# One decoder layer on one core: the shared expert's upper matrices as seven block products, and a rearranged end

## The chip, the cores and the metric

The kernel runs on one NeuronCore of one Trainium2 chip. The metric is the device time of one execution in microseconds (us), and the number that counts is the median over executions. All data are float32, but for the two operands of one small product that the reference itself rounds to eight bits; those are kept in bfloat16. Engines are named as in the profile: PE (TensorE, the matrix unit), PEld (its weight load), DVE (VectorE), ACT (ScalarE), POOL (GpSimd), SP (SyncE, which here only issues transfers).

## The reference

Inputs are `x` (4 x 512 tokens x 512 features), `ctx` (4 x 512 x 512) and weights. Three residual steps follow each other:

```python
x = x + attention(layernorm(x))     # 32 query heads, 8 key/value heads of 64, rotary, causal; wq, wk, wv, wo
x = x + xattn(layernorm(x), ctx)    # both rounded to fp8 in blocks of 128, then a 512 x 512 product per batch
x = x + ffn(layernorm(x))

def ffn(xt):                        # xt: 2048 tokens x 512;  H = 704, E = 8 experts
    probs = softmax(xt @ Wg); eidx = argmax(probs); gate = probs[eidx]
    pos = running count of earlier tokens with the same eidx; keep = pos < 256
    xd[eidx*256 + pos] = xt         # kept rows scattered into 8 x 256 slots
    oe = (silu(xd @ W1) * (xd @ W3)) @ W2           # each expert on its own 256 slots
    out = oe[eidx*256 + pos] * gate * keep          # gathered back, per token
    shared = (silu(xt @ sw1) * (xt @ sw3)) @ sw2    # every token, the "shared expert"
    return out + shared
```

The change is about the line `shared` and about the last lines of the program, in which `out` is gathered and added.

## The kernel before, in words

**Stages.** The four batches go through the attention one after another; the projections, the output product, the cross attention (jobs `c`, `s`, `t`) and the third norm with the routing (job `w`) are generators ("jobs") that a small planner, `Fill`, interleaves with the attention's own matmuls. Each job has a due step, a cost in ns of PE time, and jobs it must follow; a job yields after each piece of PE work, or with a wish to wait a while, or until DVE has room ("dve") and POOL is thought idle ("quiet"). The planner keeps a modelled time, `work.at`. All this only fixes the order in which instructions are written down; on the chip each engine runs its own list in that order, and waits for semaphores.

**Job `t`** (one tile of 128 tokens of the cross attention): DVE normalises the tile and takes block maxima (L251, L460), POOL scales it (L442), DVE rounds it in four passes (L449 to L456), PE transposes it (`ptr_h`), and four products `py` (L602) follow, each weighted by DVE (`y`, L604, in one of two buffers tagged `qm`) and added to `acc` by POOL (L597). **Job `w`**: statistics, norm, transposes (`ptr_h`, L641) with a copy to DRAM (`h3d`), the router's product `plg`, DVE's small routing arithmetic, the count product `pc`, and four indirect transfers on POOL that scatter the rows into `xd` (L719).

**Shared expert.** When the last batch's attention is done, units of the shared expert fill PE while that batch's jobs finish: `shared_up(b, c)` computes, for batch b and one block c of 128 hidden features, two products of 512 tokens over four blocks k of 128 features (8 matmuls of 128x512; block 5 holds the remaining 64 features of both matrices and has 4). ACT applies silu, DVE multiplies. `shared_down(b, j)` makes two tiles of 128 tokens of the lower product (12 matmuls of 128x512), and DVE adds them to rows `xt` that were loaded from `x2`. `between()` gives the planner a turn after every second matmul. A batch's transposed input `h3x` is loaded back from `h3d`, in two alternating buffers. The planner's loop ends when all jobs are done (L1271).

**Experts.** Expert e takes its 256 rows `xe` from `xd` (SP), transposes them, runs the same `up` on 256 columns and `down`, and stores `oe`. Weights alternate between two slots, loaded by SP behind the previous expert (the first by ACT, L1165).

**End.** In the kernel before, 27 of the shared expert's 32 units come ahead of the experts, the last of them just ahead of expert 0's first unit; the other five (three upper units, one of them the half one, and two lower ones) run behind expert 7. Sixteen gathers (L1350, POOL, one for each tile of 128 tokens) fetch the expert rows, four at a time, with a reload of `xt` from `x2` each, and DVE combines them (L1358); then SP stores the output (L1363, L1252).

PSUM has eight banks: four tagged `sp` (scores, `up`, `down` of the shared expert), one `av`, three `mm` (all jobs). A tag's banks are taken in turn, so a product waits until its predecessor in that bank has been read.

Of the kernel before, what the change touches and what calls it, by code (L numbers as in the profile page):

```python
# [14 lines left out]
P = 128  # L15
# [8 lines left out]
def decoder_layer(  # L24
# [453 lines left out]

    def pace(b):

        return 1 if b < B - 1 else 0.5

    cscales = {}

# [264 lines left out]
    for b in range(B):  # L749
        z = b * SPB  # L750
        before = [(("acc", b - 2), 0.7)] if b > 1 else []
        add(z + 5, 0, ("x", b), load(load_x, b), *before)
        if b:
            add(z - 18, 0, ("wv", b), load(load_v, b), (("q", b - 1, 11), 0.5))
            add(z - 24, 0, ("hx", b), load(load_h, b), *([(("zero",), 0.7)] if b == 1 else []))
            add(z - 22, 0, ("hs", b), job_hs(b), (("hx", b), 1))
            add(z - 16, 1760, ("h", b), job_h(b), (("hs", b), 1.5), (("q", b - 1, 4 * NG - 1), 0))
        for j in range(TB):
            if b or j:
                add(  # L760
                    z - 16, MM4, ("v", b, j), job_v(b, j), (("h", b), 0.2), (("wv", b), 1.5),
                    want=z - 4 + 0.8 * j,
                )
        for a in range(NG):
            za = z + 10 * a
            if za:
                if a == 0:
                    before = ("q", b - 1, 4 * NG - 1)
                else:
                    before = ("q", b, 4 * a - 5) if a > 1 else ("v", b, TB - 1)  # L770
                n = b * NG + a
                add(
                    za - 20, 0, ("wk", b, a), load(load_k, b, a),
                    *([(("k", *divmod(n - 2, NG)), 0.5)] if n > 2 else []),
                )
# [27 lines left out]
        before = [(("t", b - 1, j), 0) for j in range(TB)] if b else []  # L803
        add(z + 6, 220, ("cs", b), job_cs(b), *([(("w", b - 2), 0.7)] if b > 1 else []))
        add(z + (22 if b else 12), 4 * 220, ("c", b), job_c(b), (("cs", b), 0.2), *before)
        ze = z + SPB + 5
        add(ze, 0, ("s", b), job_s(b), (("o", b, NG - 1), 1))
        for j in range(TB):
            add(
                ze + 2 + (1, 3, 3, 2)[B - 1 - b] * j, 8 * 220, ("t", b, j), job_t(b, j),  # L810
                (("s", b), 0), (("c", b), 1), *([(("t", b, j - 2), 0)] if j > 1 else []),
            )
        add(ze + 9, 4 * 440 + 4000, ("w", b), job_w(b), *[(("t", b, j), 1) for j in range(TB)], *([(("cs", b + 1), 0)] if b < B - 1 else []))
    add(8, 0, ("zero",), job_zero())
    jobs.sort(key=lambda x: x.rank())
    for key in [("h", 0)]:
# [338 lines left out]
    ctx.enter_context(c_g)  # L1155
    se[1] = gp
    load_h3(1)
    slots = [gp.tile([P, WSLOT], F32, name="slot_e0")]
    evw = {}

    def job_e0():
        for evw[0] in load_ffn(slots[0], W1[0], W3[0], W2[0], bulk):
            yield -1

    add(n + 8, 0, ("e0",), job_e0())  # L1165
    jobs.sort(key=lambda x: x.rank())
    gTs, xts = {}, {}

# [33 lines left out]
    def down(gT, w2, t, name, tag, mid=None):  # L1202
# [22 lines left out]
            )  # L1225
        return pys

    def shared_up(b, c, mid=None):
        if c == 0:
            gTs[b] = gp.tile([P, NHC, T], F32, tag="gT", bufs=2, name=f"gT_{b}")  # L1230
        up(se["w"][0], h3x[b], gTs[b], c, T, f"s{b}_{c}", mid)
        if c == NHC - 1:
            se["next"] = b + 2
            load_h3(b + 2)

# [9 lines left out]
    def shared_down(b, j, mid=None):  # L1245
        for i in range(b * TB + j, b * TB + j + 2):
            xtile(i)
        for k, py in enumerate(down(gTs[b], se["w"][1], j, f"ys_{b}_{j}", "sp", mid)):
            i = b * TB + j + k
            nc.vector.tensor_tensor(xts[i], py, xts[i], ALU.add)  # L1250
            if i in routed:
                nc.sync.dma_start(out=outf[i * P : (i + 1) * P, :], in_=xts[i])  # L1252
            else:
                nc.sync.dma_start(out=x2[i * P : (i + 1) * P, :], in_=xts[i])
                routed_later.append(i)

    routed_later = []
    units = []
    for b in range(B):
        units += [(shared_up, b, c) for c in range(1 if b else 0, NHC)]  # L1260
        if b < B - 1:
            units.append((shared_up, b + 1, 0))
        units += [(shared_down, b, j) for j in range(0, TB, 2)]


    def between():
        work.at += 1720
        work.upto(n, 1e18, 2.8)

    between()  # L1270
    while jobs or work.now:  # L1271
# [3 lines left out]
        f(*args, between)  # L1275
        if se["next"] >= B - 1:
            load_h3(B - 1)
    c_am2.close()
    c_bp.close()
    c_acc.close()  # L1280

# [4 lines left out]
    def load_e(e):  # L1286
        if e < E:
            for evw[e] in load_ffn(slots[e % 2], W1[e], W3[e], W2[e], nc.sync.dma_start):
                pass

    xes, xTs, egTs = {}, {}, {}

    def load_rows(e):
        if e < E:
# [5 lines left out]

    def turn_rows(e):
        if e < E:
            xTs[e] = ep.tile([P, KC, CAP], F32, tag="xT", bufs=2, name=f"xT_{e}")
            for t in range(CT):
                nc.scalar.copy(
                    xTs[e][:, :, t * P : (t + 1) * P],
                    transpose4(xes[e, t], f"ptr_e_{e}_{t}"),
                )

    def expert_up(e, c):  # L1310
        if e < E:
            if c == 0:
                egTs[e] = ep.tile([P, NHC, CAP], F32, tag="egT", bufs=2, name=f"egT_{e}")
            up(evw[e][0], xTs[e], egTs[e], c, CAP, f"e{e}_{c}")

    load_rows(0)
    load_rows(1)
    for _ in range(3):
        f, *args = units.pop(0)
        rows_ahead(units)  # L1320
        f(*args)
    load_e(1)
    turn_rows(0)
    f, *args = units.pop(0)
    f(*args)
    expert_up(0, 0)
    for e in range(E):
        for c in range(1, NHC):
            expert_up(e, c)
            if c == 2:  # L1330
                turn_rows(e + 1)
                load_rows(e + 2)
        expert_up(e + 1, 0)
        for t, py in enumerate(down(egTs[e], evw[e][1], 0, f"epy_{e}", "mm")):
            yo = ep.tile([P, D], F32, tag="yo", bufs=2, name=f"yo_{e}_{t}")
            nc.vector.tensor_copy(yo, py)
            r0 = e * CAP + t * P
            nc.sync.dma_start(out=oe[r0 : r0 + P, :], in_=yo)
        load_e(e + 2)


    f, *args = units.pop(0)
    f(*args)

    ogs = {}

    def gather(i):
        xtile(i)
        ogs[i] = ep.tile([P, D], F32, tag="og", bufs=8, name=f"og_{i}")
        nc.gpsimd.indirect_dma_start(  # L1350
            out=ogs[i],
            out_offset=None,
# [9 lines left out]
        if last:  # L1362
            nc.sync.dma_start(out=outf[i * P : (i + 1) * P, :], in_=xts[i])  # L1363

    while units or routed_later:

        fresh = [
            (i, False)  # L1370
            for g, *a in units[1:2]
            if g is shared_down
            for i in range(a[0] * TB + a[1], a[0] * TB + a[1] + 2)
        ]
        while routed_later and len(fresh) < 4:
            i = routed_later.pop(0)
            xts.pop(i, None)
            fresh.append((i, True))
        for i, last in fresh:
            gather(i)  # L1380
        if units:
            f, *args = units.pop(0)
            f(*args)
        for i, last in fresh:
            combine(i, last)
    assert len(routed) == NT


# [58 lines left out]
```

## Time and profile before

| what | value |
|---|---|
| median of 3 runs | 1593.04 us (1593.01 to 1597.26) |
| the profiled execution's own time | 1592.05 us |
| its span in the trace | 1590.3 us (1.75 us lie around it) |
| PE busy | 1554.0 us of the span |
| DVE, ACT, POOL busy | 822.6, 515.0, 333.4 us |
| last attention product ends, first shared matmul begins | 1074.6 us |
| expert 0's first matmul | 1303.6 us |
| expert 7's last matmul ends | 1540.2 us |
| last matmul of all ends | 1577.0 us |

How to read it: a time in a row is counted from the span's start. A matmul of the program is two PE instructions (two passes over the float32 weights), so `x8` in a PE row is four matmuls. A row of the timeline gives start, duration, engine, line and operation, and in brackets how long the engine had been idle before and what ended that. In a table of windows, PEclk is the granted TensorE clock (1.00 is full).

### The profile page before, as it was taken

The page shows a single profiled execution, that of the slowest core. Times are in us where ns is not written, and L with a number is a line of the kernel's source. Part 1 is how long each engine was busy: PE and PEld are TensorE (multiplying, and loading weights), DVE is VectorE, ACT ScalarE, POOL GpSimd, SP SyncE. Part 2 cuts the span into 40 slices and gives each one's busy share as a digit, 9 for nine tenths or more (in the row PEclk, how much of TensorE's full clock was granted, in tenths as well). Part 3 has the DMA queues.
Part 4 walks back from the last instruction along what each step waited for, and adds up shares of the span by engine and source line. Part 5 has one row for each costly group of instructions (what it writes and reads, how often), then busy time and mean ns, then how long its engine had stood idle before and what let it go on. Part 6 is the DMA issues. An engine that isn't in the chain of part 4 may idle for free.

```text
span 1590.3 us, 19839 instructions
## 1 busy us (share of the span) xinstructions
PE 1554.0 (98%) x6664; PEld 853.4 (54%) x6664; DVE 822.6 (52%) x2399; ACT 515.0 (32%) x1541; POOL 333.4 (21%) x293
## 2 busy tenths in 40 slices
PE   8999999999999999999999999999999999999996
PEld 5455555545545555554555555554444557777752
DVE  4465843467776576887646686572454211111113
ACT  2354453434444444444444444441100201101100
POOL 2022301213343031333403034141132000000003
PEclk9999999999999999999999999999999999999998
DMA  4474431534325253443525423264241263556418
GB/s 140 125 225 143 100 100 30 149 100 100 99 63 153 78 140 114 100 110 93 130 61 153 131 69 83 72 204 127 77 141 66 66 205 121 157 170 232 140 61 283
DMA packets 118918, 195.32 MB, mean 123 GB/s; under 512 B 17184, under 2 KB 36640, under 8 KB 118304
## 3 DMA queue, kind: packets, MB, share of 16 engines
q10 hardware_dynamic: 65472, 100.94, 22.9%
q1 hardware_dynamic: 50784, 84.72, 17.4%
q0 software_dynamic: 2560, 8.39, 1.6%
q8 instruction: 53, 0.87, 0.2%
q14 instruction: 49, 0.40, 0.1%
HBM read 136.07 MB, written 28.57 MB: 104 GB/s over the span
## 4 chain that ended last, share of the span: by engine, by line
PE 87%; DMA 4%; DVE 3%; POOL 2%; ACT 1%; issue 1%; SPq 1%; ACTq 0%; DVEq 0%; POOLq 0%
PE py L408 14%; PE psq L308 13%; PE p_e L1181 10%; PE p_s L1181 9%; PE sc L939 8%; PE av L1020 8%; PE pt L989 7%; PE epy L1209 4%; PE psv L350 4%; PE ys L1209 3%; PE psk L308 3%; PE ptr_h L257 1%; DMA xt<-x 1%; DMA tsq<-t2q 1%; ACT pm L972 1%
## 5 line engine op out<-in xcount | busy, mean ns | idle before, releaser
L972 ACT ACTIVATE pm<-pm,mn 128x256 f32<-128x256 f32 (+3 forms) x512 | 280.9, 550 | 383.2 <-DVE mn L962 357.6
L962 DVE CUSTOM_DVE_ANT_0 pm<-sc,mask 128x256 f32<-128x256 f32 (+3 forms) x512 | 216.6, 486 | 91.0 <-PE sc L939 90.8
L408 PE MATMUL py<-wo,aT 128*128 128x512 f32 x512 | 240.3, 603 | 4.6 <-POOL aT L273 2.2
L308 PE MATMUL psq<-hT,wq 128*128 128x512 f32 x512 | 236.5, 599 | 2.3 <-DVE y L604 2.3
L1006 DVE COPY pT<-pt 128x128 f32<-128x128 f32 (+3 forms) x256 | 114.2, 485 | 114.2 <-PE pt L989 105.7
L939 PE MATMUL sc<-kT,t1q 64*128 64x384 f32 (+3 forms) x1024 | 165.8, 448 | 6.3 <-ACT pT L1000 2.5
L273 POOL TENSOR_TENSOR t1q<-t1q,tsq 128x512 f32<-128x512 f32 x64 | 83.1, 1298 | 391.8 <-DMA tsq<-t2q 214.2
L989 PEld LDWEIGHTS pt<-ident,pm 128*128 128x128 f32 x1280 | 143.7, 141 | 36.8 <-issue 27.8
L1181 PE MATMUL p_s<-h3x,slot_s 128*128 128x512 f32 x352 | 157.2, 596 | 0.0
L1181 PE MATMUL p_e<-xT,slot_e 128*128 128x256 f32 x704 | 155.1, 380 | 0.0
L989 PE MATMUL pt<-ident,pm 128*128 128x128 f32 x1280 | 154.5, 273 | 0.7 <-DVE mn L962 0.5
L1020 PE MATMUL av<-pT,v 128*64 128x512 f32 (+3 forms) x1024 | 152.4, 439 | 1.7 <-ACT pT L1000 1.7
L308 PEld LDWEIGHTS psq<-hT,wq 128*128 128x128 f32 x512 | 91.9, 190 | 102.1 <-issue 96.2
L408 PEld LDWEIGHTS py<-wo,aT 128*128 128x128 f32 x512 | 92.1, 191 | 99.7 <-issue 88.8
L1181 PEld LDWEIGHTS p_e<-xT,slot_e 128*128 128x128 f32 x704 | 132.6, 190 | 23.2 <-issue 5.8
L1000 ACT COPY pT<-pt 128x128 f32<-128x128 f32 (+3 forms) x256 | 97.1, 430 | 144.4 <-PE pt L989 114.7
L939 PEld LDWEIGHTS sc<-kT,t1q 64*128 64x128 f32 x1024 | 84.8, 186 | 87.1 <-issue 58.4
L1020 PEld LDWEIGHTS av<-pT,v 128*64 128x64 f32 x1024 | 68.3, 136 | 108.3 <-issue 96.2
L273 POOL TENSOR_TENSOR acc<-acc,y 128x512 f32<-128x512 f32 x64 | 80.9, 1269 | 180.6 <-DVE y L604 148.8
L1181 PEld LDWEIGHTS p_s<-h3x,slot_s 128*128 128x128 f32 x352 | 65.1, 190 | 74.8 <-issue 73.1
L972 ACT ACTIVATION_READ_ACCUMULATOR pm<-pm,mn 128x1 f32 x512 | 95.6, 187 | 0.0
L273 POOL TENSOR_TENSOR aT<-aT,rrb 128x512 f32<-128x512 f32 x64 | 81.0, 1296 | 30.5 <-DMA rrb<-rrd 30.5
(172 smaller groups left out, 1355.0 us busy)
## 6 DMA issues: line engine op xcount, KB each, us to landing
slot_e<-in_L_ffn_W_dram SPq DMA_DIRECT2D x14, 1280.0 KB
wq<-in_L_attn_wq_dram ACTq DMA_DIRECT2D x16, 1024.0 KB
tsq<-t2q SPq DMA_DIRECT2D x256, 64.0 KB
wo<-in_L_attn_wo_dram ACTq DMA_DIRECT2D x16, 1024.0 KB
rrb<-rrd ACTq DMA_DIRECT2D x32, 512.0 KB
slot_e<-in_L_ffn_W_dram SPq DMA_DIRECT2D x7, 1408.0 KB
kT<-t1k ACTq DMA_DIRECT2D x64, 128.0 KB
xt<-x SPq DMA_DIRECT2D x28, 256.0 KB
```

What stands on the lines that cost most here:

```text
L273: nc.gpsimd.tensor_tensor(*args)
L308: nc.tensor.matmul(ps, w[:, k, c0 : c0 + P], hTs[b][:, k, :], start=(k == 0), stop=(k == KC - 1),)
L408: nc.tensor.matmul(py, aT[:, r, j * P : (j + 1) * P], wts["o", a][:, r, :], start=(r == 0), stop=(r == 3),)
L939: nc.tensor.matmul(scs[g][:, o : o + nk], qTs[b, p][g * HD : (g + 1) * HD, it * P : nk], kTs[b, p // 2][g * HD : (g + 1) * HD, 0:nk], star ...
L962: nc.vector.tensor_tensor_reduce(out=pm[:, o : o + nk], in0=scs[g][:, o : o + nk], in1=mask[:, T - nk : T], scale=-(HD**-0.5), scalar=3.0e ...
L972: nc.scalar.activation(pm[:, o : o + nk], pm[:, o : o + nk], AF.Exp, bias=mn, scale=-1.0, accum_out=rss[b, a][:, col : col + 1],)
L989: nc.tensor.transpose(pt[:, j * P : (j + 1) * P], pms[g][:, j * P : (j + 1) * P], ident)
L1000: nc.scalar.copy(pT[:, 0 : it + 1, it * P : nk], pt[:, o : o + nk].rearrange("p (j t) -> p j t", t=P),)
L1006: nc.vector.tensor_copy(pT[:, it + 1, 0:nk], pt[:, o : o + nk])
L1020: nc.tensor.matmul(av[g * HD : (g + 1) * HD, j * P : T], vs[b][:, j, v0 : v0 + HD], rhs, start=(j == 0), stop=(j == TB - 1),)
L1181: nc.tensor.matmul(pp[:, 0:cols], w13[:, k, o : o + P], xT[:, k, 0:cols], start=(k == 0), stop=(k == KC - 1),)
L1209: nc.tensor.matmul(py, gT[:, c, (t + i) * P : (t + i + 1) * P], w2[:, c, :], start=(c == 0), stop=False,)
```

## The change

**1. Seven products instead of eight.** For batches 1 to 3 and hidden blocks 0 to 4 (15 chunks), `up7` replaces `up`. The two weight matrices' columns of the chunk (w1 on top, w3 below) and the two halves of the features make a 2 x 2 block matrix A; the features' halves and the tokens' halves make a 2 x 2 block matrix B. Strassen's scheme in Winograd's form gives the four blocks of A·B from seven products of blocks and sums of blocks. Each product is two matmuls of 128x256. The weight sums (s1 to s4, four POOL subtractions or additions of 2x128 columns per block) are made once, behind batch 0's use of the block; s1 overwrites a part of the weights. The token sums (t1 to t4, four POOL operations of 2x256) are made per batch, in `shared_down(b - 1, 0)`. Of the outputs, ACT copies two from PSUM, DVE makes five additions with a PSUM operand, POOL two additions of 256 columns and the final product of 512; silu is applied to the two halves.

**2. Order.** Block 5 of a batch now comes between its predecessor's two lower units. Of the lower units only the last three run behind expert 7; the upper ones are all ahead of the experts. The slot of expert 0's weights moves to where attention buffers were, and is loaded once the last output product is done. In the expert stage the transposed rows and the products live in parts of `h3x` and `wS`, which are free by then.

**3. End.** All `xt` rows are fetched ahead of expert 7's lower product, into buffers that are free; the 16 gathers go to POOL in a row behind the first lower unit's matmuls; the gathered rows go into the free weight slot.

**4. Planner.** In the last batch the jobs' wishes to wait are 0.3 of the others' instead of 0.5, the jobs `s` and `t` are due five steps earlier and the first two tiles at once; job `w` is due four steps earlier in all batches, which shifts a few matmuls in the attention's order too.

```diff
-        return 1 if b < B - 1 else 0.5
+        return 1 if b < B - 1 else 0.3
...
-        ze = z + SPB + 5
+        ze = z + SPB + (5 if b < B - 1 else 0)
...
-                ze + 2 + (1, 3, 3, 2)[B - 1 - b] * j, 8 * 220, ("t", b, j), job_t(b, j),
+                ze + 2 + (0, 3, 3, 2)[B - 1 - b] * j, 8 * 220, ("t", b, j), job_t(b, j),
...
-        add(ze + 9, 4 * 440 + 4000, ("w", b), job_w(b), *[(("t", b, j), 1) for j in range(TB)], *([(("cs", b + 1), 0)] if b < B - 1 else []))
+        add(ze + 5, 4 * 440 + 4000, ("w", b), job_w(b), *[(("t", b, j), 1) for j in range(TB)], *([(("cs", b + 1), 0)] if b < B - 1 else []))
...
+    def weight_sums(c):
+        a11, a12, a21, a22 = blocks(c)
+        s2, s3, s4 = (wS[:, i, :, c * P : (c + 1) * P] for i in range(3))
+        gpsimd(0.66, s3, a11, a21, ALU.subtract)
+        gpsimd(0.66, a21, a21, a22, ALU.add)
+        gpsimd(0.66, s2, a21, a11, ALU.subtract)
+        gpsimd(0.66, s4, a12, s2, ALU.subtract)
+
+    def token_sums(b):
+        x = h3x[b]
+        b11, b12, b21, b22 = (x[:, k : k + 2, t : t + T2] for k in (0, 2) for t in (0, T2))
+        t1, t2, t3, t4 = (xSs[:, i] for i in range(4))
+        gpsimd(1.27, t1, b12, b11, ALU.subtract)
+        gpsimd(1.27, t3, b22, b12, ALU.subtract)
+        gpsimd(1.27, t2, b22, t1, ALU.subtract)
+        gpsimd(1.27, t4, b21, t2, ALU.subtract)
+        xS[b] = t1, t2, t3, t4, b11, b21, b22
+
+    def up7(b, c, mid):
...
+        def product(i, w, x):
+            ps = bank("av" if i == 3 else "sp", f"p7_{b}_{c}_{i}")[:, 0:T2]
+            for k in range(2):
+                nc.tensor.matmul(ps, w[:, k, :], x[:, k, :], start=k == 0, stop=k == 1)
+            return ps
...
+        nc.scalar.copy(p1, product(0, a11, b11))
+        nc.vector.tensor_tensor(u2, product(1, s2, t2), p1, ALU.add)
+        nc.vector.tensor_tensor(u3, product(2, s3, t3), u2, ALU.add)
+        if mid:
+            mid(2500, 1.3)
+        nc.scalar.copy(p5, product(3, s1, t1))
+        gpsimd(0.66, u2, u2, p5, ALU.add)
+        gpsimd(0.66, c2[:, T2:T], u3, p5, ALU.add)
+        nc.vector.tensor_tensor(g[:, 0:T2], product(4, a12, b21), p1, ALU.add)
+        nc.scalar.activation(g[:, 0:T2], g[:, 0:T2], AF.Silu)
+        if mid:
+            mid(1700)
+        nc.vector.tensor_tensor(g[:, T2:T], product(5, s4, b22), u2, ALU.add)
+        nc.scalar.activation(g[:, T2:T], g[:, T2:T], AF.Silu)
+        nc.vector.tensor_tensor(c2[:, 0:T2], product(6, a22, t4), u3, ALU.add)
+        gpsimd(1.27, g, g, c2, ALU.mult)
+        if mid:
+            mid(1700, 1.0)
...
+    units = [u for u in ups if u[2] == HF] + downs[:-3] + [u for u in ups if u[2] < HF]
...
+        if e == E - 1:
+            rows_back()
...
+    for n, (f, *args) in enumerate(units):
+        f(*args)
+        if n == 0:
+            for i in first + tiles[0] + tiles[2] + tiles[1]:
+                gather(i)
+            for i in first + tiles[0]:
+                combine(i, True)
+        if n == 1:
+            for i in tiles[2]:
+                combine(i, False)
+            for i in tiles[1]:
+                combine(i, True)
```

More of the change, by code (lines that the diff above doesn't have):

```diff
@@ L1157, in decoder_layer @@
     load_h3(1)
-    slots = [gp.tile([P, WSLOT], F32, name="slot_e0")]
-    evw = {}
+    slots, evw = [], {}
     def job_e0():
+        c_am2.close()
+        c, pool = space("e0p", "right")
+        ctx.enter_context(c)
+        slots.append(pool.tile([P, WSLOT], F32, name="slot_e0"))
         for evw[0] in load_ffn(slots[0], W1[0], W3[0], W2[0], bulk):
             yield -1
-    add(n + 8, 0, ("e0",), job_e0())
+    add(n + 8, 0, ("e0",), job_e0(), (("o", B - 1, NG - 1), 0.1))
     jobs.sort(key=lambda x: x.rank())
@@ L1226, in down, with blocks @@
         return pys
+    T2 = T // 2
+    wS = gp.tile([P, 3, 2, HF * P], F32, name="wS")
+    xSs = gp.tile([P, 4, 2, T2], F32, name="xS")
+    xS = {}
+    def blocks(c):
+        w, cols = se["w"][0], slice(c * P, (c + 1) * P)
+        low = slice(H + HT + c * P, H + HT + (c + 1) * P)
+        return w[:, 0:2, cols], w[:, 2:4, cols], w[:, 0:2, low], w[:, 2:4, low]
+    def weight_sums(c):
[5 more added lines that the diff above has]
+        gpsimd(0.66, s4, a12, s2, ALU.subtract)
@@ new lines, in token_sums, with part @@
+    def token_sums(b):
[8 more added lines that the diff above has]
+    def up7(b, c, mid):
+        a11, a12, s1, a22 = blocks(c)
+        s2, s3, s4 = (wS[:, i, :, c * P : (c + 1) * P] for i in range(3))
+        t1, t2, t3, t4, b11, b21, b22 = xS[b]
+        def product(i, w, x):
[3 more added lines that the diff above has]
+            return ps
+        def part(tag, bufs=2):
+            return gp.tile([P, T2], F32, tag=tag, bufs=bufs, name=f"{tag}_{b}_{c}")
+        g = gTs[b][:, c, :]
+        p1, p5, u2, u3 = part("p1"), part("p5", 1), part("u2"), part("u3")
+        c2 = gp.tile([P, T], F32, tag="c2", bufs=2, name=f"c2_{b}_{c}")
+        nc.scalar.copy(p1, product(0, a11, b11))
[16 more added lines that the diff above has]
+            mid(1700, 1.0)
@@ L1228, in shared_up @@
     def shared_up(b, c, mid=None):
-        if c == 0:
+        if b not in gTs:
             gTs[b] = gp.tile([P, NHC, T], F32, tag="gT", bufs=2, name=f"gT_{b}")
-        up(se["w"][0], h3x[b], gTs[b], c, T, f"s{b}_{c}", mid)
-        if c == NHC - 1:
+        if b and c < HF:
+            up7(b, c, mid)
+        else:
+            up(se["w"][0], h3x[b], gTs[b], c, T, f"s{b}_{c}", mid)
+        if not b and c < HF:
+            weight_sums(c)
+        if c == (HF - 1 if b else HF):
             se["next"] = b + 2
@@ L1252, in shared_down, with between @@
                 nc.sync.dma_start(out=outf[i * P : (i + 1) * P, :], in_=xts[i])
-            else:
+            elif i not in kept:
                 nc.sync.dma_start(out=x2[i * P : (i + 1) * P, :], in_=xts[i])
-                routed_later.append(i)
-    routed_later = []
+        if j == 0 and b < B - 1:
+            token_sums(b + 1)
+    kept = set()
     units = []
     for b in range(B):
-        units += [(shared_up, b, c) for c in range(1 if b else 0, NHC)]
+        units += [(shared_up, b, c) for c in range(HF if b else NHC)]
+        units += [(shared_down, b, j) for j in range(0, TB, 2)]
         if b < B - 1:
[L1262 to L1268, printed above, removed]
+            units.insert(-1, (shared_up, b + 1, HF))
+    def between(ns=1720, room=2.8):
+        work.at += ns
+        work.upto(n, 1e18, room)
     between()
@@ L1277, in decoder_layer @@
             load_h3(B - 1)
-    c_am2.close()
     c_bp.close()
@@ L1291, in decoder_layer @@
     xes, xTs, egTs = {}, {}, {}
+    wS_flat = wS.rearrange("p i k c -> p (i k c)")
     def load_rows(e):
@@ L1302, in turn_rows @@
         if e < E:
-            xTs[e] = ep.tile([P, KC, CAP], F32, tag="xT", bufs=2, name=f"xT_{e}")
+            xTs[e] = h3x[B - 2][:, e % 2 * 2 : e % 2 * 2 + 2, :].rearrange(
+                "p a (c t) -> p (a c) t", t=CAP
+            )
             for t in range(CT):
@@ L1312, in expert_up, with rows_back @@
             if c == 0:
-                egTs[e] = ep.tile([P, NHC, CAP], F32, tag="egT", bufs=2, name=f"egT_{e}")
+                lo = e % 2 * NHC * CAP
+                egTs[e] = wS_flat[:, lo : lo + NHC * CAP].rearrange("p (c t) -> p c t", c=NHC)
             up(evw[e][0], xTs[e], egTs[e], c, CAP, f"e{e}_{c}")
     load_rows(0)
+    load_e(1)
     load_rows(1)
-    for _ in range(3):
-        f, *args = units.pop(0)
-        rows_ahead(units)
+    ups = [u for u in units if u[0] is shared_up]
+    downs = [u for u in units if u[0] is shared_down]
+    units = [u for u in ups if u[2] == HF] + downs[:-3] + [u for u in ups if u[2] < HF]
+    for i, (f, *args) in enumerate(units):
+        if i == len(units) - 1:
+            turn_rows(0)
+        rows_ahead(units[i + 1 :])
         f(*args)
[L1322 to L1325, printed above, removed]
     expert_up(0, 0)
+    units = downs[-3:]
+    tiles = [[b * TB + j, b * TB + j + 1] for _, b, j in units]
+    for pair in tiles:
+        kept.update(pair)
+    first = [i for i in range(NT) if i not in kept]
+    spare = [h3x[B - 1][:, k, :] for k in range(KC)]
+    spare += [xSs.rearrange("p i k t -> p (i k t)")[:, k * D : (k + 1) * D] for k in range(4)]
+    spare += [wS_flat[:, k * D : (k + 1) * D] for k in range(NHC * CAP // D)]
+    def rows_back():
+        for i in first:
+            xts[i] = spare.pop(0)
+            nc.sync.dma_start(out=xts[i], in_=x2[i * P : (i + 1) * P, :])
+        for i in tiles[0] + tiles[1] + tiles[2]:
+            xtile(i)
     for e in range(E):
@@ L1339, in decoder_layer @@
         load_e(e + 2)
-    f, *args = units.pop(0)
-    f(*args)
     ogs = {}
@@ L1348, in gather @@
         xtile(i)
-        ogs[i] = ep.tile([P, D], F32, tag="og", bufs=8, name=f"og_{i}")
+        ogs[i] = slots[E % 2][:, i * D : (i + 1) * D]
         nc.gpsimd.indirect_dma_start(
@@ L1363, in combine @@
             nc.sync.dma_start(out=outf[i * P : (i + 1) * P, :], in_=xts[i])
[L1367 to L1385, printed above, removed]
+    for n, (f, *args) in enumerate(units):
[10 more added lines that the diff above has]
+                combine(i, True)
     assert len(routed) == NT
```

## The prediction

> **What bounds the kernel now.** I read the page's first two parts, then the table of windows by stage.
>
> ```profile
> span 1590.3 us, 19839 instructions
> PE 1554.0 (98%) x6664; PEld 853.4 (54%) x6664; DVE 822.6 (52%) x2399; ACT 515.0 (32%) x1541; POOL 333.4 (21%) x293
> PE   8999999999999999999999999999999999999996
> ```
> ```profile
> 1050.00:1100.00 50.00, 46.11 (x199) 24.32 (x198) 23.73 (x65) 13.89 (x32) 9.89 (x9) 0.97 0.76 230
> 1150.00:1200.00 50.00, 50.00 (x140) 21.74 (x139) 25.88 (x48) 5.22 (x9) 15.73 (x14) 1.00 0.36 117
> 1550.00:1590.00 40.00, 27.04 (x66) 11.16 (x64) 15.43 (x23) 1.19 (x2) 13.52 (x14) 0.90 0.84 282
> ```
> The first number behind the width is PE's busy time: PE is the bound. From 1100 to 1577 us it never waits (50.00 of 50 in each window); 3.89 us are lost in 1050 to 1100 and 13.3 us behind the last matmul. So each PE microsecond saved between is time saved, and each PE wait added is time lost. The chain of waits shows the end:
>
> ```profile
> 1540.19 13.95 PE p_s L1181 x32
> ...
> 1559.86 5.95 DMA xt<-x
> ...
> 1571.34 6.15 DMA xt<-x
> ...
> 1581.22 3.97 DMA xt<-x
> ...
> 1585.38 0.75 DVE xt L1358
> ```
> Reloads of `xt`, 4 to 6 us each, are the last chain, not PE.
>
> **The change, part by part.** The order of instructions is read from the changed program; durations are rows of before.
>
> *Seven products.* A 128x512 chunk costs 16 passes; 40 passes of `p_s` from 1176.42 to 1193.59 took 17.17 us, so 6.87 us a chunk. A 128x256 pass is seen in the experts: 56 of `p_e` in 12.09 us, 0.216 us, where the 0.190 us weight load just hides. 28 passes are 6.05 us. The other bound is half a wide pass, 0.2146 us (6.01). I take the first: 15 x 0.825 = **−12.4 us**.
>
> *Does a chunk keep PE fed?* The nearest rows:
>
> ```profile
> L1193 DVE TENSOR_TENSOR egT<-p_e,egT 128x256 f32<-128x256 f32 x40 | 17.0, 425 | 119.2 <-PE p_e L1181 119.2
> L1192 ACT ACTIVATE egT<-p_e 128x256 f32<-128x256 f32 x40 | 15.3, 383 | 167.2 <-PE p_e L1181 167.2
> L273 POOL TENSOR_TENSOR acc<-acc,y 128x512 f32<-128x512 f32 x64 | 80.9, 1269 | 180.6 <-DVE y L604 148.8
> ```
> Products end every 0.86 us. The fourth ends at 3.45; ACT's copy (0.38) and POOL's addition (between half of 1.27 and all of it; I take 0.65, as the time goes with the columns in the 128x256 and 128x512 rows of DVE, 425 and 690 ns) make u2 at 4.65, at worst 5.25. The sixth product ends at 5.18, its DVE addition at 5.65, and its bank is wanted at 7.77. There are 2.1 us of room at either price, so 0 for a chunk alone. POOL has 2.6 us of work per 6.05 us. Weight sums (20 x 0.65) and token sums (12 x 1.27) lie where POOL is mostly idle (3.86 of 50 us in 1100 to 1150).
>
> *Where other jobs stand in these queues*, PE does wait. Count from the last `py` of the output product.
> (a) Tiles 0 and 1 of the last batch now go through job `t` together. Their `y` use two buffers, and POOL's list is acc00, acc10, acc01, acc02, acc11, acc12, a scatter, acc03, acc13, so DVE's `y` and POOL's additions take turns: first `y` at 39.4, then 1.27 a step with the scatter's 1.0, last `y` at 55.5. The eighth `py` waits for its bank: 1.35 us. Behind the last `y` DVE has two normalisations with block maxima (3.6 us, as POOL is adding during the first), and only then the addition that frees the bank of the third product of chunk (1, 0): it comes at 59.9, PE is there at 55.3: 4.55 us. Bounds: 0, as in the same stage of before, and 9 if each takes twice that.
> (b) In chunk (2, 1) DVE's norm root (13 small operations, 2.5 us) and one normalisation stand between two bank-freeing additions: 3.1 us against 2.1 us of room: 1.1 us.
> (c) The last batch's four scatters stand ahead of chunk (3, 0)'s POOL additions:
>
> ```profile
> 1265.73 1.01 POOL L719 DMA_INDIRECT xd<-h,r_dst_i  x1 [54.61 <-DVE r_flat L715]
> 1268.75 0.96 POOL L719 DMA_INDIRECT xd<-h,r_dst_i  x1 [2.01 <-DMA xd<-h,r_dst_i]
> ```
> Each waits for the one before: 3 us a step, 9.9 us in all. From the end of batch 2's upper part: indices at 13.7, POOL free at 23.6, u2 at 24.3, DVE's addition at 24.75, the bank wanted at 22.0: 2.75 us. Behind this POOL list waits only DVE's same addition; the experts' `xe` loads come 12 us ahead of need.
>
> *The clock.* A wait costs more than itself:
>
> ```profile
> 1090.49 3.68 PE L408 MATMUL py<-wo,aT 128*128 128x512 f32 x4 [2.20 <-POOL aT L273]
> 1088.00:1090.00 2.00, 0.28 (x5) 0.11 (x2) 0.09 (x1) 0.58 (x1) 0.83 (x1) 1.00 1.00 286
> 1090.00:1092.00 2.00, 1.51 (x2) 0.71 (x3) 0.00 (x0) 0.00 (x0) 2.00 (x3) 0.65 0.06 17
> 1092.00:1094.00 2.00, 2.00 (x4) 0.69 (x3) 0.00 (x0) 0.00 (x0) 2.00 (x2) 0.50 0.00 0
> ```
> After 2.2 us of idling the granted clock fell to half for some 3.3 us: 1.6 us lost. The 1.68 us gap at 1070 cost no clock. I count one fall, behind (a): 1.6. Added waits: 1.35 + 4.55 + 1.6 + 1.1 + 2.75 = **+11.35 us**.
>
> The Trainium skill's "TensorE: Matmul & The Clock Gate", Part 1, speaks of half clock after an idle window of about 3.4 us; the row shows a fall after 2.2 us. If the page held, (c) would cost no clock and the sum would stay as it is; by the row (c) may cost 1.6 us more.
>
> *A wait that goes.* The 2.2 us above is for POOL's `aT`. In the changed order `plg` and a transpose (1.28 us) come ahead of that product and `ptr_c` (0.22) behind, so the wait is near 1.1 us, and too short for a fall: **−2.1 us** (1.1 of waiting, 1.0 of the clock, the rest being POOL's pace of 1.27).
>
> *The end.* Let X be the end of expert 7's lower product (1540.2 in before). Before: 2.5 upper and 2 lower units follow, PE ends at X + 36.8, the span at X + 50.1. After: three lower units of 9.8 us, PE ends at X + 29.5; the upper work moved ahead of X is the same PE time. The stores of `oe` no longer share the DMA engines with reloads (before, gathers began at X + 7.0); I take X + 4.5. Gathers went every 1.25 us in before, so the sixteenth is issued at X + 24.2; 16 gathers and 16 stores are 8.4 MB, 21 us at the 397 GB/s seen at the end and 30 us at the 282 of the window's mean (1550 to 1590 us), ends at X + 26 to X + 34. I take the first, as no reload is left. Then the last chain is PE, two DVE additions (1.3 us), and what lay behind the last DVE operation in before (1590.3 − 1586.1 = 4.2): 5.7 us behind PE instead of 13.3: **−7.6 us**, at worst 0.
>
> *SBUF port.* A normalisation took 2.09 us at 1175.48, beside POOL's additions, and 0.54 at 1144.87 without. The Trainium skill's "SBUF — State Buffer", Who interferes with whom, says that a VectorE operation with two SBUF inputs or in a two-port mode and a GpSimd operation shut each other out. That speaks against more POOL work here; by it the rounding of tiles 2 and 3, inside chunks, would be 3.7 us each instead of 2.4, 1.6 us over the room, and the sum 3.2 us more. The chunk's own additions have one operand in PSUM and are spared by it.
>
> *Sum.* 1592.05 − 12.4 + 11.35 − 2.1 − 7.6 = 1581.3 us for an execution like the profiled one. The median is 1.0 us above it, so **1582 us**. Shifts of single matmuls in the attention I put at 0: it has 15 us of PE idling in 950 us.
>
> **Rivals.**
> A, the waits are hidden as in before (for it: 50.00 of 50 in every window; against: before had one POOL instruction where now several stand): 1571 us.
> B, tiles 2 and 3 clump as tiles 0 and 1 do, 4.55 + 1.6 more (for: same buffers; against: their POOL list alternates, and PE has 10 us of lower units there): 1588 us.
> C, slower: POOL's two additions per chunk come late in all 15 chunks, so that each wait passes 2.1 us of room and each pulls the clock down, 1.5 + 1.6 us a chunk, 46 us: 1571 + 46 = 1617 us. It decides from nine such chunks; against it speaks u2's room, which needs POOL's addition at 3.1 us instead of 0.65.
> D, nothing comes of the seven products because weights change every 0.216 us and loads need 0.190: at 0.245 us a pass the gain is gone: 1594 us. Against it are the experts' rows.
>
> **How the numbers follow.** Forecast 0.48, A 0.20, B 0.14, C 0.11, D 0.07. The measurement can tell 0.3% (4.8 us): faster is below 1588.3, slower above 1597.8. Half of B lies on either side of the lower bound: faster 0.75, same 0.14, slower 0.11. The range goes from A to B with (c)'s clock and the port's 3.2: 1571 to 1591.
>
> **What would show it.** PE's rows of the seven products: 28 passes in 6.05 us. Waits of PE on DVE of about 4.5 us in the third product of (1, 0), 1 us in (2, 2), 3 us in (3, 1), and PEclk below 1 behind the first. No `xt` reload in the last chain, and some 5.7 us from the last matmul to the end. Wrong if PE waits within ordinary chunks, or if the gathers end behind PE.

## The result and the profile after

The changed kernel's median is 1594.39 us (1587.93 to 1601.0, 20 runs), that of the kernel before 1593.38 us (1590.03 to 1597.4, 20 runs): ratio 1.0006, 95% interval 0.9994 to 1.0017. No change, where 1582 us was forecast. The profiled execution of the changed kernel took 1587.93 us, the shortest of its 20, so its trace shows less of the loss than is typical. Its page:

```profile
span 1586.2 us, 20493 instructions
PE 1545.7 (97%) x6839; PEld 888.4 (56%) x6844; DVE 849.8 (54%) x2459; ACT 529.5 (33%) x1586; POOL 405.1 (26%) x370
```

PE is busy 8.3 us less (1554.0 before; 3.8 us more up to the first shared product, 12.1 less from there on) and waits 40.5 us instead of 36.3. The table of windows tells where; the first row is the kernel before, in the stretch of the attention that I did not show in the prediction.

```profile
50.00:1000.00 950.00, 935.26 (x4420) 494.23 (x4418) 620.05 (x1867) 407.30 (x1279) 249.56 (x203) 1.00 0.42 112
```

The same view of the changed kernel:

```profile
50.00:1000.00 950.00, 927.78 (x4360) 490.71 (x4366) 609.43 (x1841) 402.27 (x1263) 245.62 (x199) 1.00 0.40 110
1050.00:1100.00 50.00, 48.02 (x224) 25.26 (x223) 29.04 (x83) 17.36 (x46) 14.23 (x13) 1.00 0.81 243
1150.00:1200.00 50.00, 47.06 (x185) 31.11 (x184) 34.33 (x61) 8.13 (x19) 30.14 (x28) 1.00 0.44 148
1250.00:1300.00 50.00, 46.87 (x210) 35.38 (x209) 16.43 (x56) 12.12 (x26) 20.93 (x22) 1.00 0.40 130
```

PE, the first number behind the width, waits 22.2 us in the attention instead of 14.7. The shared stage, which had no wait at all from 1100 us on, now has 2.94 and 3.13 us in two windows. Those two I had forecast; the 7.5 us in the attention I had not.

The easiest way to place the loss is to cut each trace at two marks: the first shared product, and the experts' first product. Up to the first mark both kernels do the same work, in a different order. Between the two marks they do not: the kernel before makes 27 of the shared expert's 32 units there, the changed one 29, so that column and the last one compare kernels only within the old order of units (before, e2, e9) or within the new one (the others). "Clock" sums, over windows of 2 us, the width times what the granted clock lacked of 1.

| trace | first shared product | PE idle to there | clock to there | from there to the experts | clock there | experts to end |
|---|---|---|---|---|---|---|
| before | 1074.6 | 20.9 | 1.7 | 228.8 | 1.7 | 286.9 |
| changed | 1085.3 | 27.8 | 3.4 | 229.0 | 0 | 271.9 |
| changed, second trace (e4) | 1094.9 | 28.9 | 11.9 | 232.6 | 3.4 | 272.3 |
| e1, old attention | 1076.1 | 20.9 | 3.4 | 233.6 | 5.1 | 272.6 |
| e2, before with job `w` moved | 1089.4 | 28.1 | 5.1 | 229.6 | 1.7 | 287.4 |
| e3, eight products | 1073.8 | 20.1 | 1.7 | 233.3 | 0 | 273.0 |
| e5 | 1073.9 | 20.3 | 1.7 | 226.4 | 0 | 272.3 |
| e6 | 1073.9 | 20.1 | 1.7 | 225.2 | 0 | 271.6 |
| e7, batch 0's `w` moved | 1079.5 | 23.3 | 1.7 | 231.2 | 0 | 272.1 |
| e8, batch 2's `w` moved | 1079.5 | 22.5 | 3.4 | 231.4 | 3.4 | 274.2 |
| e9, before with two `w` moved | 1081.0 | 25.8 | 3.4 | 233.1 | 5.1 | 288.0 |

From the first mark to the end the changed kernel gained 14.8 us (515.7 to 500.9). Before the mark it lost 10.7, and 20.3 in its second trace.

**The end** took the time that was forecast. Its chain of waits:

```profile
1569.72 1.11 PE ys L1222 x4
...
1573.85 0.95 POOL slot_e L1455
1574.79 0.30 issue
1575.10 5.83 DMA slot_e<-oe,gidx
...
1582.37 0.60 DVE xt L1329
```

No reload of `xt` is left. The last gather is issued 24.0 us behind the end of expert 7's lower product (1550.0 + 1.1) and lands at 1580.9, and PE's last matmul ends at 1580.6. So the gathers end 29.8 us behind that product, where 26 was taken and 34 was the other bound, and 0.3 us behind PE: the chain goes through them and not through PE, which costs no more than those 0.3 us. The span ends 5.6 us behind PE; 13.3 before, 5.7 forecast.

**The seven products** in PE's timeline (in brackets: how long PE had been idle, and what ended that):

```profile
1170.55 1.13 PE L1274 MATMUL p<-h3x,slot_s 128*128 128x256 f32 x4
1171.52 1.03 PE L1274 MATMUL p<-xS,wS 128*128 128x256 f32 x4
1175.11 1.13 PE L1274 MATMUL p<-xS,wS 128*128 128x256 f32 x4 [2.57 <-DVE xt L1329]
1176.08 1.03 PE L1274 MATMUL p<-xS,slot_s 128*128 128x256 f32 x4
...
1179.53 1.03 PE L1274 MATMUL p<-h3x,slot_s 128*128 128x256 f32 x4
...
1185.58 1.03 PE L1274 MATMUL p<-h3x,slot_s 128*128 128x256 f32 x4
...
1244.39 1.13 PE L1274 MATMUL p<-xS,wS 128*128 128x256 f32 x4 [0.72 <-DVE gT L1295]
...
1290.91 1.13 PE L1274 MATMUL p<-xS,wS 128*128 128x256 f32 x4 [3.13 <-DVE gT L1295]
```

An undisturbed chunk takes 1185.58 − 1179.53 = 6.05 us. A product behind a wait takes some 0.1 us longer (1176.08 − 1175.11 = 0.97 us, against 0.86), and one behind another job's matmuls is a little longer too. Over all 15 chunks, from each matmul's start to the next one's and without the waits, PE spent 92.3 us on the seven products, and 103.6 us on the eight in the kernel before: 11.3 us less, not 12.4. The three waits stand at the three products that the prediction named: the third of chunk (1, 0), the third of (2, 2), the third of (3, 1).

### The profile page after: what moved, and what is told of

It reads as the page before. It is cut to its first block, busy times and chain, and to the rows that moved or that the text cites. A ratio compares the mean times of both kernels' runs of the same rounds, so it can differ in the third digit from the quotient of the medians.

```text
span 1586.2 us, 20493 instructions
## 1 busy us (share of the span) xinstructions
PE 1545.7 (97%) x6839; PEld 888.4 (56%) x6844; DVE 849.8 (54%) x2459; ACT 529.5 (33%) x1586; POOL 405.1 (26%) x370
## 4 chain that ended last, share of the span: by engine, by line
PE 84%; DVE 5%; DMA 5%; POOL 2%; ACT 2%; issue 2%; SPq 1%; ACTq 0%; POOLq 0%; DVEq 0%
PE py L408 13%; PE psq L308 12%; PE p_e L1184 10%; PE sc L939 8%; PE av L1020 8%; PE pt L989 7%; PE p L1274 5%; PE epy L1212 4%; PE psv L350 4%; PE ys L1212 3%; PE psk L308 3%; PE p_s L1184 2%; DMA rrb<-rrd 1%; ACT pm L972 1%; PE ptr_h L257 1%
## 5 line engine op out<-in xcount | busy, mean ns | idle before, releaser
L939 PE MATMUL sc<-kT,t1q 64*128 64x384 f32 (+3 forms) x1024 | 169.2, 450 | 10.8 <-DVE pT L1006 3.5
L1184 PE MATMUL p_e<-h3x,slot_e 128*128 128x256 f32 x704 | 155.1, 380 | 0.0
L308 PEld LDWEIGHTS psq<-hT,wq 128*128 128x128 f32 x512 | 92.3, 191 | 102.2 <-issue 97.7
L1184 PEld LDWEIGHTS p_e<-h3x,slot_e 128*128 128x128 f32 x704 | 132.6, 190 | 22.8 <-issue 5.3
L1196 DVE TENSOR_TENSOR wS<-p_e,wS 128x256 f32<-128x256 f32 x40 | 17.0, 424 | 119.3 <-PE p_e L1184 119.3
L1455 POOL DMA_INDIRECT slot_e<-oe,gidx x16 | 15.9, 996 | 243.7 <-DMA oe<-yo 239.1
```

The source lines that it names most:

```text
L308: nc.tensor.matmul(ps, w[:, k, c0 : c0 + P], hTs[b][:, k, :], start=(k == 0), stop=(k == KC - 1),)
L939: nc.tensor.matmul(scs[g][:, o : o + nk], qTs[b, p][g * HD : (g + 1) * HD, it * P : nk], kTs[b, p // 2][g * HD : (g + 1) * HD, 0:nk], star ...
L1184: nc.tensor.matmul(pp[:, 0:cols], w13[:, k, o : o + P], xT[:, k, 0:cols], start=(k == 0), stop=(k == KC - 1),)
```

## The experiments

**Is it the attention, or the new stage?** The planner's part of the change moves the due step of job `w` in every batch. Of the changed kernel's edits, this one alone alters the order of PE's instructions ahead of the first shared product.

e1 gives batches 0 to 2 the old due step:

```diff
-        add(ze + 5, 4 * 440 + 4000, ("w", b), ...
+        add(ze + (9 if b < B - 1 else 5), 4 * 440 + 4000, ("w", b), ...
```

> The changed kernel, but job w of batches 0 to 2 is due where it was before, so that PE's order up to the first shared product is the one of before, instruction for instruction. Theory 1 (the moved due step of job w cost the attention some 11 us, and the shared stage and the end gained some 15): first shared product at about 1075 us instead of 1085, what follows as in the changed kernel (about 501 us), 1577 us profiled, median 1576 to 1582, ratio near 0.991. Theory 2 (the attention differs by the chance of one execution, and the typical run of the changed kernel loses its time in the new shared stage): median 1592 to 1596, ratio 0.998 to 1.002.

e2 makes the opposite edit in the kernel before:

```diff
-        add(ze + 9, 4 * 440 + 4000, ("w", b), ...
+        add(ze + (5 if b < B - 1 else 9), 4 * 440 + 4000, ("w", b), ...
```

> The kernel before, with only the due step of job w of batches 0 to 2 moved as the change moves it, so that PE's order up to the first shared product is the one of the changed kernel. Theory 1: first shared product at about 1085 us or later, median 1602 to 1609, ratio 1.006 to 1.010. Theory 2: median 1591 to 1595, ratio within 0.998 to 1.002.

e4 runs the changed kernel again, for a second trace:

> The changed kernel itself, for the trace of a second execution. Theory 1: the first shared product begins at 1082 us or later, and from there to the end it takes 499 to 503 us. Theory 2: the first shared product begins between 1073 and 1079 us, and from there it takes over 510 us, with more or longer waits of PE in the chunks of seven products.

e1: median 1580.23 us (before on the same chip 1593.2), ratio 0.9914 (0.9895 to 0.9932). e2: 1609.12 us, ratio 1.0104 (1.0081 to 1.0126). The first shared product of e1, in PE's timeline:

```profile
1076.12 3.70 PE L1184 MATMUL p_s<-h3x,slot_s 128*128 128x512 f32 x8
```

Theory 2 falls, on both sides. In the traces PE's 4976 matmul instructions ahead of the first shared product come in one order in before and in e1, and in another one in the changed kernel and in e2 (of which the changed kernel's first trace lacks 5 records). The two orders agree for 1277 instructions, up to some 287 us, and part there: more than the few shifted matmuls that "The change" speaks of. The due step alone costs the kernel before 15.9 us, and the changed kernel without it is 13.0 us faster than before. In the second trace of the changed kernel (1601.48 us) the first shared product begins at 1094.9 us, and from there it takes 504.9 us: 1.9 us over theory 1's 503, with 3.4 us of clock lost behind two of the three waits.

**Which part of the attention?** e7 and e8 move job `w` of one batch in e1:

```diff
+        add(ze + (5 if b in (0, B - 1) else 9), ...    # e7; e8: (2, B - 1)
```

> The kernel of the first run with the due step of job w moved in batch 0 alone (5 instead of 9). If the loss in the attention is made of single places, this keeps the waits of the changed kernel's trace up to 650 us, the one of 3.27 us at 631 us with its fall of the clock among them, and drops the one of 2.51 us at 924 us: the second batch's attention starts some 6 us later than in the first run, and the median is 5 to 10 us above the first run's (1585 to 1590). Rival (the attention's loss is one of the last batches, or of all alike): within 2 us of the first run or above 1592.

> The same with batch 2 alone: it keeps the wait of 2.51 us at 924 us with its fall of the clock and drops those up to 650 us: 4 to 6 us above the first run, 1584 to 1587; with the run before it, the two parts add up to the 14 us between the first run and the changed kernel. Rival: no part of it, within 2 us of the first run.

> The kernel before with the due step of job w moved in batches 0 and 1. PE's order is that of the changed kernel up to some 905 us, so the wait of 3.27 us at 631 us, which was gone in the run with batch 0 alone, is back, with its fall of the clock; the one of 2.51 us at 924 us is not there. If the rest of the loss (14.2 less 2.9 and 5.7, so 5.6 us) is batch 1's: 8 to 10 us above the kernel before, 1601 to 1604. Rival (it comes only where batch 2 moves as well): 3 us above, 1595 to 1598.

e7: 1583.13 us, 2.9 above e1, below what was expected: the wait of 3.27 us at 631 us was not in its trace, so batch 0's move alone does not make it. e8: 1585.88 us, 5.7 above e1, as expected; its trace keeps the wait ahead of the last batch's scores, and the clock falls to 0.51 behind it:

```profile
918.22 1.97 PE L939 MATMUL sc<-kT,t1q 64*128 64x128 f32 x8 [2.51 <-issue]
```

e9, the kernel before with `w` of batches 0 and 1 moved, took 1602.76 us (before 1593.03, ratio 1.0051, 1.0034 to 1.0067): 9.7 us, as expected, and the wait is back. PE's timeline:

```profile
632.11 3.38 PE L989 MATMUL pt<-ident,pm 128*128 128x128 f32 x16 [3.21 <-DVE mn L962]
```

Batches 0 and 1 cost 9.7 us (in the kernel before), batch 2 another 5.7 (in the changed one), and all three together 15.9 (in the kernel before). The sizes for e7 and e8 are rough: e1 ran on another chip, and by the ratios to before (0.9928 and 0.9944 against e1's 0.9914), whose intervals overlap e1's, they are 2.2 and 4.8 us. That each move costs something shows in their traces too, where the first shared product begins at 1079.5 us, 3.4 behind e1 and 5.6 behind e5 and e6, which have the old attention as well. Much of the loss stands at two places: in the changed kernel's first trace the waits of 3.27 and 2.51 us are 4.4 us more than before has there (none and 1.37), and the clock fell behind both, 3.4 us. What such a place looks like shows in DVE's timeline. The changed kernel:

```profile
624.61 0.16 DVE L238 TENSOR_SCALAR veb<-mvb 128x4 f32<-128x4 f32 x1
...
625.87 1.26 DVE L245 TENSOR_TENSOR r0b<-veb,rsb 128x4 f32<-128x4 f32 x1
...
628.14 0.69 DVE L317 TENSOR_TENSOR t2q<-psq,rt 128x512 f32<-128x512 f32 x1
...
629.61 0.45 DVE L251 TENSOR_SCALAR h<-acc,mvb,rsb 128x512 f32<-128x512 f32 x1
630.09 0.69 DVE L460 TENSOR_REDUCE am<-h 128x4 f32<-128x512 f32 x1
630.69 0.28 DVE L962 CUSTOM_DVE_ANT_0 pm<-sc,mask 128x128 f32<-128x128 f32 x1
```

The same place of the kernel before:

```profile
626.00 0.34 DVE L368 RECIPROCAL rr<-rs 128x32 f32<-128x32 f32 x1
626.26 0.23 DVE L962 CUSTOM_DVE_ANT_0 pm<-sc,mask 128x128 f32<-128x128 f32 x1
...
630.80 0.16 DVE L238 TENSOR_SCALAR veb<-mvb 128x4 f32<-128x4 f32 x1
```

`pm<-sc` masks the scores, and PE's transposes `pt` need it. In before DVE masks first (626.26) and begins the chain of small operations for the norm's root (L238 to L247) afterwards, at 630.80. In the changed order that chain, 3.5 us, and a normalisation with block maxima, 1.1 us, stand ahead of the mask, and PE waits 3.27 us for it:

```profile
631.51 3.37 PE L989 MATMUL pt<-ident,pm 128*128 128x128 f32 x16 [3.27 <-DVE mn L962]
```

In before the same transposes follow without a wait:

```profile
628.19 1.97 PE L989 MATMUL pt<-ident,pm 128*128 128x128 f32 x16
```

Nothing of job `w` is in these rows: the planner laid out everything behind the moved due step anew, and jobs `s` and `t` fell on another place. That DVE's order makes this wait is read from the rows; no run moved the mask alone. Ahead of the last batch's scores, by contrast, the chain and the normalisation stand before the mask in both kernels: there PE waited 1.37 us in before and 2.51 in the changed order. Then the clock at the first of these places, in 2 us windows of the changed kernel (third number from the end of a row):

```profile
630.00:632.00 2.00, 0.49 (x3) 0.49 (x4) 1.97 (x9) 0.99 (x3) 0.00 (x0) 0.75 0.47 106
632.00:634.00 2.00, 2.00 (x11) 2.00 (x11) 2.00 (x7) 2.00 (x9) 1.09 (x1) 0.50 0.11 26
```

**What are the seven products worth?** e3 is e1 with the eight products in all chunks:

```diff
-        if b and c < HF:
-            up7(b, c, mid)
-        else:
-            up(se["w"][0], h3x[b], gTs[b], c, T, f"s{b}_{c}", mid)
-        if not b and c < HF:
-            weight_sums(c)
+        up(se["w"][0], h3x[b], gTs[b], c, T, f"s{b}_{c}", mid)
...
-        if j == 0 and b < B - 1:
-            token_sums(b + 1)
```

(The second part of the edit takes out the token sums. A third one, not shown, lets the units that are left when the planner's loop ends run in the order of their list, with the last three lower units still behind expert 7.)

> The kernel of the first run with the old eight products in all chunks, without the weight sums and token sums; the new order and the new end stay. PE has 15 x 0.83 = 12.4 us more, and the three waits of PE behind the seven products (2.57, 0.72, 3.13 us in the changed kernel's trace) go. Theory 1: 6 us above the first run, 1582 to 1588. Rival (the seven products gain nothing, for what they save in passes they lose in waits and clock): the same as the first run or faster.

e3: 1583.76 us (1581.61 to 1584.83), ratio 0.9936 (0.9918 to 0.9954): 3.5 us above e1, in the lower part of the expected range, though under the 6 expected. The waits of PE in its trace from the first shared product on:

```profile
PE py L408 <- POOL aT L273: 0.8, 2, 0.5
```

The same view of e1:

```profile
PE p L1274 <- DVE gT L1295: 4.2, 2, 3.5
PE p L1274 <- DVE xt L1329: 2.6, 1, 2.6
...
PE py L408 <- POOL aT L273: 0.3, 1, 0.3
PE py L602 <- DVE y L604: 0.2, 1, 0.2
```

The seven products bring 11.3 us less of PE's work, against 6.8 us of waits and what these pull down of the clock (5.1 us in this trace, none in the changed kernel's first). So I took the waits away.

e5: in chunk (3, 0) DVE makes the two additions that stood behind POOL's scatters.

```diff
-        gpsimd(0.66, u2, u2, p5, ALU.add)
-        gpsimd(0.66, c2[:, T2:T], u3, p5, ALU.add)
+        if (b, c) == (B - 1, 0):
+            nc.vector.tensor_tensor(u2, u2, p5, ALU.add)
+            nc.vector.tensor_tensor(c2[:, T2:T], u3, p5, ALU.add)
+        else:
+            gpsimd(0.66, u2, u2, p5, ALU.add)
+            gpsimd(0.66, c2[:, T2:T], u3, p5, ALU.add)
```

> The kernel of the first run, but in chunk (3, 0) the two additions of p5 go to DVE instead of POOL, where they stood behind the last batch's four scatters. My step (c): the wait of PE in the third product of chunk (3, 1), 3.5 us in the first run's trace, goes, and with it the fall of the clock at 1282 to 1290 us (some 3 us lost there in that trace, none in the changed kernel's first trace): 3 to 6 us below the first run, median 1574 to 1578. Rival: the wait moves to the next bank (POOL's product g*c2 or chunk (3, 1)'s own additions are late too), and the median stays at 1580.

e6: also, block 5 of batch 1 behind both lower units of batch 0.

```diff
-            units.insert(-1, (shared_up, b + 1, HF))
+            units.insert(-1 if b else len(units), (shared_up, b + 1, HF))
```

> As the run before, and block 5 of batch 1 goes behind both lower units of batch 0, so that DVE's additions that free the banks of ys_2_0 and ys_2_1 stand ahead of the two normalisations. My step (a): the wait of 2.6 us in the third product of chunk (1, 0) goes: 2.6 to 4.3 us below the run before, median 1570 to 1575. Rival: the normalisations now stand between additions of chunk (1, 0) or (1, 1), at 3.3 us beside POOL (as in the changed kernel's trace at 1169 us) they pass the room of 2.1 us, and PE waits 1 to 2.5 us there instead: no gain or under 1 us.

e5: 1577.54 us, ratio 0.9894 (0.9869 to 0.9918); e6: 1573.91 us, ratio 0.9873 (0.9849 to 0.9897), before on their chip 1593.75. e5 is 2.7 us below e1, whose chip had before at 1593.2 (its median as expected, the step just under the 3 expected); the intervals of the two ratios overlap, so it is the trace that settles it: e5's has no wait at chunk (3, 1). e6 is 3.6 below e5, as expected. Neither rival held. e6's waits of PE from the first shared product on:

```profile
PE py L408 <- POOL aT L273: 2.4, 4, 1.2
PE p L1274 <- DVE gT L1299: 0.7, 1, 0.7
PE p L1274 <- DVE gT L1203: 0.4, 1, 0.4
```

Both long waits are gone. e6 is the fastest of all these kernels, some 20 us below before and the changed kernel, and 9.9 us below e3 with its eight products: of the 12.4 us that the prediction put on the seven products, 9.9 are then kept.

## Why the prediction was wrong

The step that failed: "Shifts of single matmuls in the attention I put at 0: it has 15 us of PE idling in 950 us." The order of the attention is worth far more than that: its changed due step cost 15.9 us in the kernel before (e2) and 14.2 in the changed one (1594.39 − 1580.23). The argument was wrong in kind: the 15 us were what a good order had left, not a bound on what another one can cost. No term of the sum stood for it, and no rival either: the waits of rivals B and C lie in the shared stage. Rival D's 1594 us is the measured median, but by luck: it let the seven products gain nothing, and they gained. Of the first trace's 10.7 us, 6.9 are waits of PE and 1.7 clock; the other 2 lie in stretches that count as busy, and stay open.

The upper end of the range was mis-added as well: rival B with the clock of (c) and the 3.2 us of the port is 1588 + 1.6 + 3.2 = 1592.8 us, not 1591, and the measured median lies above either.

The rest of the sum, tested by e1 (1580.2 us against the 1582 forecast), held better, in part because its errors offset each other:

- *Seven products, −12.4*: 6.05 us in an undisturbed chunk, as forecast, but −11.3 over all 15. At 92.3 us for 420 passes, 0.220 us each, rival D's 0.245 did not occur.
- *(a) the y stage, 1.35 + 4.55 + 1.6 of clock*: the place was right, the size too high. The eighth `py` waited 0.24 us, the third product 2.57, and the clock fell behind it in two of six traces. The eight `y` came within 11.2 us (1157.43 to 1168.64 from first to last start) where I had laid out 16.1, as the last of them needs the buffer that POOL's sixth addition frees, and the scatter comes behind that. With block 5 moved (e6) no wait is left at the third product.
- *(b) 1.1*: 0.72. *(c) 2.75*: 3.0 to 3.5 us in five traces, and e5 shows the cause: with the additions off POOL the wait is gone. I had counted no clock for it; by the row of before I had said that it could cost 1.6 more. It fell in three of five traces, and cost 1.7 us in one and 3.4 in two.
- *The wait that goes, −2.1*: 2.20 us became 0.28 in the first trace and 0.9 in the second, and the fall of the clock behind it went: together 3.6 us in the first trace, more than forecast.
- *The end, −7.6*: 13.3 us became 5.6, −7.7 (the prediction's two parts, 1.3 and 4.2, add up to 5.5).

Waits in the shared stage sum to 6.7 us instead of 9.75, without the clock. The first trace's terms, −11.3 + 6.7 − 3.6 − 7.7, make −15.9 us, where 14.8 were gained; the last 1.1 us stay open. Rival A (all hidden) was wrong as stated, rival B too: tiles 2 and 3 made no wait. That the forecast's gain is there and is paid for elsewhere is shown, by e1 and e2 with the same edit in both directions.

## What to carry to other kernels

Where a planner writes the order of a long stage, a due step is not a small edit: compare the order of every engine's list in the stages that the change does not mean to touch, and keep that order unless it is part of what is tried. Here one constant undid seven products and a shorter end. Look not only at the engine that is the bound: at 631 us the order of DVE's list, which is busy about half of the time, decided when PE's operand was ready. And try each part of a bundle by itself; the part that nobody prices may be the costly one.

## What the runs showed of the hardware

**The length of a wait does not settle whether the clock falls.** A wait of 1.46 us at 356 us left the clock at 1.00 in the kernel before:

```profile
356.00:358.00 2.00, 1.16 (x8) 0.92 (x9) 1.93 (x7) 1.41 (x5) 1.48 (x2) 1.00 0.00 0
358.00:360.00 2.00, 1.89 (x14) 0.98 (x13) 2.00 (x10) 1.11 (x5) 0.31 (x1) 1.00 0.05 12
```

and halved it in e1, at the same wait of 1.46 us:

```profile
356.00:358.00 2.00, 1.71 (x10) 1.30 (x10) 1.93 (x8) 0.86 (x3) 1.24 (x2) 0.89 0.04 8
358.00:360.00 2.00, 2.00 (x8) 0.92 (x6) 1.63 (x11) 1.66 (x7) 0.00 (x0) 0.50 0.02 4
```

Over the eleven traces that place, with 1.2 to 1.5 us of waiting, fell in six; the 2.6 us in chunk (1, 0) in two of six; the 3.0 to 3.5 us in chunk (3, 1) in three of five; the 2.5 us before the last batch's scores in four of four, and the 3.2 us at 631 us in four of four. A wait of 2.0 to 2.4 us at some 588 us, which six traces have, was followed by a fall in e5 alone. So the place counts, and at some places the execution. One fall costs about 1.7 us where no wait follows it closely, 3.4 behind chunk (3, 1) in e1 and e8. In the second trace of the changed kernel the waits that followed kept the clock at half from 640 to 650 us, some 5 us lost, in an execution of 1601.48 us. The Trainium skill, "TensorE: Matmul & The Clock Gate", Part 1, describes a free-running window of some 3.4 us in which activity is watched, with results that vary from run to run. Falls that come in one execution and not in another fit that; falls after waits of 1.2 to 2.5 us do not fit an idle window of that whole length.

**A VectorE operation can wait behind a row of GpSimd's.** DVE's normalisation and, before it, a product of only 128x16, in the changed kernel:

```profile
1149.90 0.17 DVE L583 TENSOR_TENSOR sxw<-sf_c,sf_x 128x16 f32<-128x16 f32 x1
...
1152.23 3.96 DVE L583 TENSOR_TENSOR sxw<-sf_c,sf_x 128x16 f32<-128x16 f32 x1
...
1169.25 3.31 DVE L251 TENSOR_SCALAR h<-acc,mvb,rsb 128x512 f32<-128x512 f32 x1
...
1173.20 0.54 DVE L251 TENSOR_SCALAR h<-acc,mvb,rsb 128x512 f32<-128x512 f32 x1
```

POOL in the same time:

```profile
1152.44 2.49 POOL L273 TENSOR_TENSOR xS<-h3x 128x512 f32<-128x512 f32 x2
1154.89 2.61 POOL L273 TENSOR_TENSOR xS<-h3x,xS 128x512 f32<-128x512 f32 x2
...
1169.78 2.49 POOL L273 TENSOR_TENSOR acc<-acc,y 128x512 f32<-128x512 f32 x2
```

L251 takes 0.54 us alone and 3.31 beside two additions of POOL, until the second is done. The 128x16 product takes 0.17 us alone, and 3.96 beside POOL's four token sums: it ends at 1156.2 us, where the third of them ends by the mean of its pair, and not with the row (1157.5). I had counted 2.09 us for the normalisation from before's trace; beside several operations in a row it can be the length of two or three of them. The Trainium skill, "SBUF — State Buffer", Who interferes with whom, calls the shared port an exclusive lock; that DVE stands still beside POOL agrees, and here it did so for more than one of POOL's operations. That POOL is the reason is read from the times; no run took POOL's work away there.
